# Scaling one weight on ScalarE instead of VectorE, in a kernel of five chained stages

## The chip, the cores and the metric

The kernel runs on one core of a Trainium2 chip. A core has five engines with an instruction queue each, and each of them works through its queue in order: TensorE (PE in the profile) multiplies matrices, VectorE (DVE) and ScalarE (ACT) work elementwise and also read the product banks (PSUM), GpSimd (POOL) works elementwise on the on-chip memory (SBUF) and issues gathers, and SyncE (SP) issues the other transfers (DMAs). Engines wait for one another through semaphores.

The metric is the time of one execution in microseconds (us); less is better. Before the change it is 2020.08 us, the median of three runs (2018.74 to 2021.53).

## What is computed

The reference takes `x` of shape 2 x 2048 x 512 (two sequences, 2048 tokens, 512 channels), all in float32, and adds two residual branches. Cut to what matters here:

```
y  = clip((x * style) @ weight.T * dcoef + bias)      # stage 1, modulated linear layer
hs = recurrence(rms_norm(y), 4 projections) + y       # stage 2, gated linear recurrence
up = gelu(rms_norm(hs) @ mlp_gate.T) * (rms_norm(hs) @ mlp_fc.T)   # stage 3, width 1536
x2 = x + up @ out_w.T + hs                            # stage 4, "down"
w  = softmax(aw)                                      # six weights
cat = [w0*h, w1*t, w2*m, w3*n, w4*r, w5*s]            # six branches of x2, 512 channels each
h1 = silu(cat @ int_W1 + b1)                          # stage 5, first product
q  = int8(layer_norm(h1 @ int_W2 + b2))
out = x2 + (q @ int8(rhs)) * scales
```

`h`, `t` and `s` are layer norms of `x2` with gains and offsets picked by table lookups (`h` by a gather from a table of 500 rows). `m`, `n` and `r` are `x2` plus a vector for each sequence. The six factors of the softmax are multiplied into the six 512 x 512 blocks of `int_W1` once, and not into the activations.

## The kernel before, in words

The channels lie on the 128 partitions, in chunks of 128, the tokens along the free axis. Stages 1 to 4 work on slices of 1024 tokens (four slices), stage 5 on blocks of 512 tokens (eight blocks).

**A product in seven steps.** Each large product is cut into 2 x 2 blocks and done with seven block products instead of eight (Strassen's scheme in Winograd's form). A weight tile therefore holds seven slots: four loaded quarters (0 to 3), and three sums, which `combine` (L121 to L126) makes on GpSimd in four operations. The operand's blocks `B11`, `B21`, `B12` and `B22` are likewise overwritten by sums, on VectorE, at L222. `paired_in_place` (L176) writes out the order of the steps for stages 4 and 5. A step is named here by the slot of the weights that it uses. For stage 4 the order is: step 0 with `B11` into bank pair `a`, step 1 with `B21` into `b`, step 6 with `B22` into `d`, step 4 with the old `B11` into `d`, step 5 with the new `B22`, step 2 with `B12` and step 3 with the new `B21`, these last three into `a`. Between step 6 and step 4 the program gives VectorE the sum `B22 = B22 - B11`, which overwrites what step 6 reads and which step 5 needs, and after step 4 the sum `B21 = B21 - B22`.

**Stage 4, `down(s, then)` (L899), for `s` = 0 to 3.** Its four operands `op_11`, `op_21`, `op_12` and `op_22` are large tiles (128 x 3072) that are loaded anew for each slice. Three of them lie in memory zones (A, B and C) that stage 5 takes over: zone A is `op_11`, zone B is `op_12`, zone C is `op_22`. `tap` (L920) keeps partial results: after step 6, ScalarE copies the two banks of `d` into `dk` tiles (L925), and VectorE subtracts them from the residual (L929). The argument `then` hangs other work behind single steps: the small products of the conditioning vectors, and the preparation of stage 5's weights.

**The weights of stage 5's first product.** `raw(k)` (L1209) loads a 512 x 512 block of `int_W1` whole, and `quarters(first, second)` (L1215) loads two blocks into the slots of two seven-slot tiles, with eight DMAs of 256 KB on SP (L1223). Both call `scaled(k, rhs)` (L1193), which multiplies a block by its softmax factor in four VectorE instructions of 128 x 512 (L1195). Blocks 3 and 4 are loaded raw. `quarters(2, 1)` makes the first combined weight (`w_int`, for `x2` and the time branch), to which blocks 3 and 4 are added on GpSimd (L1246). The last combined weight is `quarters(5, 0)`, called from `second_weight` (L1252), which hangs behind step 4 of the last `down` (`then[3]`: `then` counts the steps in their order from 0, and step 4 is the fourth). It takes the buffers that the raw blocks 3 and 4 leave, so its loads wait for L1246.

**What comes after.** When the last `down` no longer needs a tile, the first block of stage 5 takes its place: `load(0)` (L1356) loads the block's activations into zone A (L1358), TensorE transposes them (`tr_x`, L1383) between the last steps of `down`, ScalarE copies the transposes out (L1386), VectorE forms means and variances (L1320) and the norm (L1334). GpSimd issues four gathers from the table of 500 rows (L1363), two of them into zone B. VectorE then applies the gathered gains (L1408, L1409), and TensorE begins the first product of stage 5 (`ps_h_a`).

Instructions are queued on each engine by a scheduler in the order that it finds from the program and its priorities, except where the order is written out or `tc.issue_after(ins)` places an instruction behind another one on its own engine.

Of the kernel before, what the change touches and what calls it, by code (L numbers as in the profile page):

```python
# [11 lines left out]
AF = mybir.ActivationFunctionType  # L12
ALU = mybir.AluOpType
# [37 lines left out]
def adaln_attn_ffn(ctx: ExitStack, tc: tile.TileContext, a: dict, out: bass.AP):  # L51
    nc = tc.nc
# [11 lines left out]
    def col(name, k=0, n=1):  # L64
        at = _COL[name] + k
        return cols[:, at : at + n]
# [15 lines left out]
    wsm = const.tile([P, 6], FP, name="wsm")  # L82
# [25 lines left out]
    held = {}  # L108
# [12 lines left out]
    def combine(w):  # L121

        nc.gpsimd.tensor_add(w[:, 4], w[:, 2], w[:, 3])
        nc.gpsimd.tensor_sub(w[:, 5], w[:, 4], w[:, 0])
        nc.gpsimd.tensor_sub(w[:, 2], w[:, 0], w[:, 2])
        nc.gpsimd.tensor_sub(w[:, 6], w[:, 1], w[:, 5])  # L126

    def by_chunks(w):
        return w.rearrange("(c p) o -> p c o", p=P)
# [766 lines left out]
    def tmp(name):  # L896
        return dp.tile([P, T], FP, tag="k", name=name, bufs=8)

    def down(s, then=()):  # L899
        b, t0 = divmod(s, PER_S)  # L900
        b11, b21, b12, b22 = op
        for k, t in ((0, b11), (1, b12), (3, b22), (2, b21)):
            nc.sync.dma_start(t, pp_d[s][:, k])

        res = []
        for o in range(C):
            t = dp.tile([P, S], FP, tag="res", name=f"res_{s}_{o}", bufs=4)
            nc.sync.dma_start(t, hs_d[s][:, o, :])
            for k, half in enumerate((a_, b_)):
                x = xr[2 * (o % 2) + k]  # L910
                nc.sync.dma_start(x, by_chunks(a["xT"][b])[:, o, ts(2 * t0 + k, T)])
                nc.vector.scalar_tensor_tensor(
                    t[:, half], t[:, half], col("L0_attn_out_b", o), x, ALU.add, ALU.add
                )
            res.append(t)

        def pair(f):
            return lambda *x: [f(u, *(y[u] if y is not None else None for y in x)) for u in (0, 1)]

        def tap(n, ps, less):  # L920
            kept = []
            for u in (0, 1):
                t = tmp(f"dk{n}")
                if n == 4:
                    nc.scalar.copy(t, ps[u])  # L925
                else:
                    o, half = {1: (u, a_), 2: (u, b_), 3: (u + 2, b_)}[n]
                    if less:
                        nc.vector.tensor_sub(less[u], res[o][:, half], less[u])  # L929
                        nc.vector.tensor_add(t, ps[u], less[u])  # L930
                    else:
                        nc.vector.tensor_add(t, ps[u], res[o][:, half])
                kept.append(t)
            return kept

        def store(o, half, ps, other):
            nc.vector.tensor_add(other, ps, other)
            nc.sync.dma_start(scratch[2 * s + (half is b_)][:, o, :], other)

        return paired_in_place(  # L940
            w_dn, [b11], [b21], [b12], [b22],
            lambda n: [
                (d_ps if n == "d" else ab_ps).tile([P, T], FP, tag="s", name=f"dn_{s}_{n}{u}")
                for u in (0, 1)
            ], tap,
            pair(lambda u, ps, kept: store(u, a_, ps, kept)),
            pair(lambda u, ps, kept: store(u, b_, ps, kept)),
            pair(lambda u, ps: store(u + 2, a_, ps, res[u + 2][:, a_])),
            pair(lambda u, ps, kept: store(u + 2, b_, ps, kept)), then,
        )  # L950
# [237 lines left out]
    def block_of(k):  # L1188
        return a["int_W1"][k * D : (k + 1) * D, :].rearrange("(c p) o -> p c o", p=P)

    bias = w3.tile([P, D], FP, name="bias", bufs=1)

    def scaled(k, rhs):  # L1193
        for c in range(C):
            nc.vector.tensor_scalar(rhs(c), rhs(c), wsm[:, k : k + 1], None, ALU.mult)  # L1195

    def vectors(of):

# [10 lines left out]
    def raw(k):  # L1209
        w = w14(f"int_w1_{k}")  # L1210
        nc.sync.dma_start(w[:, 0:C], block_of(k))
        scaled(k, lambda c: w[:, c, :])
        return w

    def quarters(first, second):  # L1215


        ws = [w3.tile([P, 7, 2, 2 * P], FP, tag="w", name=f"w_int_{first}_{g}") for g in (0, 1)]
        views = []
        for at, k in enumerate((first, second)):  # L1220
            for g in (0, 1):
                for h in (0, 1):
                    nc.sync.dma_start(  # L1223
                        ws[g][:, 2 * h + at],
                        block_of(k)[:, 2 * g : 2 * g + 2, ts(h, 2 * P)],
                    )
            views.append(lambda c, at=at: ws[c // 2][:, at : at + 3 : 2, c % 2, :])
            scaled(k, views[-1])
        return ws, views[0]

    def vectors_as_operands(w):
# [5 lines left out]
    w3_4 = [raw(3), raw(4)]  # L1237
    vectors_as_operands(w3_4[0])
    w_int, of_x = quarters(2, 1)
    of_34 = [lambda c, w=w: w[:, c, :] for w in w3_4]  # L1240

# [8 lines left out]
            combine(w)  # L1250

    def second_weight():  # L1252
        ws, _ = quarters(5, 0)
        for w in ws:
            combine(w)
        w_int.extend(ws)
# [99 lines left out]
    def load(i):  # L1356
        x2T = block("x2T", i)
        nc.sync.dma_start(x2T, scratch[i])  # L1358
        return {"x2T": x2T}
# [265 lines left out]
    with tc.high_priority():  # L1625
        k = load(0)
# [64 lines left out]
    for i in range(NB):  # L1691
# [27 lines left out]
        last, k = k, nxt  # L1719
# [68 lines left out]
```

## Time and profile before

| what | us |
|---|---|
| median of three runs | 2020.08 |
| time of the profiled execution | 2021.65 |
| its span, first to last instruction | 2019.9 |
| TensorE busy in the span | 2001.7 (99%) |
| VectorE busy | 1174.8 (58%) |
| ScalarE busy | 653.4 (32%) |
| GpSimd busy | 153.8 (8%) |
| mean granted TensorE clock | 0.996 |

The profile shows one execution. "Busy" counts the time in which an engine had an instruction at work; the figures of TensorE are modelled for pipelined matmuls, and busy does not mean full speed. The granted clock is the share of full speed that TensorE was given. A row of a timeline names the start, the duration, the engine, the line, the operation, the tiles and the count; in brackets stands how long the engine had been idle before it, and what ended that. A row with a count covers several instructions. A float32 matmul of 128 x 512 shows as two records of some 0.43 us each, so that a step of `down`, twelve matmuls, is 24 records and some 10.3 us.

The stretch that the change touches is the last call of `down`, from about 1320 us to 1395 us of the span:

| engine | from 1331 us to 1352 us | from 1352 us to 1370 us |
|---|---|---|
| TensorE | steps 6 and 4 into `dn_d` | waits, then step 5 into `dn_a` |
| VectorE | scalings of the last weight, one L929 | two operand sums (L222), one L929 |
| ScalarE | two copies of `dn_d` (L925) | nothing |
| GpSimd | additions to the first weight (L1246), its `combine` | `combine` of the last weight |
| SP | loads of the last weight (L1223) | load into zone A (L1358), stores of results |

### The profile page before, as it was taken

The numbers are of one execution on the slowest core, as the hardware profiler recorded it, in microseconds if no ns is written. First come the engines' busy times: TensorE is split into PE (matmuls) and PEld (weight loads), VectorE is DVE, ScalarE is ACT, GpSimd is POOL, SyncE is SP. The second block draws the span as 40 slices with busy tenths as digits, with TensorE's granted clock in tenths as the row PEclk, the third lists the DMA queues.
The fourth block names the chain that finished last, engine by engine and source line by source line (L and its number), as shares of the span: only waits on it lengthen the run. The fifth ranks groups of instructions, "written<-read, shape, count | busy, mean of one in ns | idle before, by whom it ended". The sixth has DMA issues, their size and how long they took to land.

```text
span 2019.9 us, 16905 instructions
## 1 busy us (share of the span) xinstructions
PE 2001.7 (99%) x6292; PEld 1067.4 (53%) x6300; DVE 1174.8 (58%) x1783; ACT 653.4 (32%) x863; POOL 153.8 (8%) x127
## 2 busy tenths in 40 slices
PE   9999999999999999999999999989999999999998
PEld 5444444444444444444444444435877777777774
DVE  6667666666534224324325465466687687687675
ACT  4557777777522222222221000001302302302301
POOL 0141000000400000000010000061300000000000
PEclk9999999999999999999999999999999999999999
DMA  5661212121512112111335766533211211211110
GB/s 202 217 198 52 90 62 98 42 94 58 161 42 91 45 42 94 42 42 52 110 112 180 229 220 224 201 111 130 92 45 63 76 51 63 73 53 63 32 32 21
DMA packets 99332, 197.21 MB, mean 98 GB/s; under 512 B 21393, under 2 KB 49591, under 8 KB 95153
## 3 DMA queue, kind: packets, MB, share of 16 engines
q1 hardware_dynamic: 94584, 179.31, 26.4%
q0 software_dynamic: 4608, 16.78, 2.5%
q8 instruction: 50, 0.82, 0.2%
q14 instruction: 34, 0.27, 0.0%
q10 hardware_dynamic: 56, 0.03, 0.0%
HBM read 133.27 MB, written 58.75 MB: 95 GB/s over the span
## 4 chain that ended last, share of the span: by engine, by line
PE 95%; DVE 1%; issue 1%; POOL 1%; DMA 1%; ACT 0%; SPq 0%; POOLq 0%; ACTq 0%; DVEq 0%
PE up_a L134 16%; PE ps_h_a L134 11%; PE rec_a L134 11%; PE up_d L134 8%; PE dn_a L134 7%; PE ps_h_d L134 6%; PE rec_d L134 5%; PE ps_o L1524 5%; PE up_b L134 4%; PE dn_d L134 3%; PE ps_h_b L134 3%; PE y_a L134 3%; PE rec_b L134 3%; PE dn_b L134 2%; PE y_d L134 1%; PE ps_f L1548 1%
## 5 line engine op out<-in xcount | busy, mean ns | idle before, releaser
L134 PE MATMUL dn_a<-op,w_dn 128*128 128x512 f32 x384 | 169.7, 600 | 5.3 <-DVE op L222 5.3
L134 PE MATMUL up_a<-h,w_up 128*128 128x512 f32 x384 | 172.6, 592 | 0.0
L814 DVE SCALAR_TENSOR_TENSOR prod<-up_d,cols,k 128x512 f32<-128x512 f32 x48 | 36.0, 751 | 199.6 <-ACT k L297 199.6
L297 ACT COPY k<-up_a 128x512 f32<-128x512 f32 x144 | 84.0, 584 | 196.8 <-PE up_a L134 196.7
L794 ACT ACTIVATE gate<-gate,cols 128x512 f32<-128x512 f32 x96 | 68.8, 721 | 215.3 <-DVE gate L793 213.3
L134 PE MATMUL up_a<-h2T,w_up 128*128 128x512 f32 x288 | 129.5, 592 | 0.0
L134 PEld LDWEIGHTS dn_a<-op,w_dn 128*128 128x128 f32 x384 | 72.9, 192 | 95.8 <-issue 87.9
L134 PEld LDWEIGHTS up_a<-h,w_up 128*128 128x128 f32 x384 | 72.9, 190 | 91.9 <-issue 89.7
L134 PE MATMUL rec_a<-h,w_rec 128*128 128x512 f32 x256 | 115.1, 592 | 0.0
L134 PE MATMUL rec_a<-hT,w_rec 128*128 128x512 f32 x256 | 115.1, 592 | 0.0
L1524 PE MATMUL ps_o<-int_w,h 128*128 128x512 f32 x224 | 103.6, 605 | 0.0
L134 PEld LDWEIGHTS up_a<-h2T,w_up 128*128 128x128 f32 x288 | 54.7, 190 | 68.9 <-issue 68.9
L134 PE MATMUL up_b<-h,w_up 128*128 128x512 f32 x192 | 86.3, 592 | 0.0
L134 PE MATMUL up_d<-h,w_up 128*128 128x512 f32 x192 | 86.3, 592 | 0.0
L134 PE MATMUL dn_d<-op,w_dn 128*128 128x512 f32 x192 | 83.7, 594 | 0.0
L134 PEld LDWEIGHTS rec_a<-h,w_rec 128*128 128x128 f32 x256 | 48.6, 190 | 61.2 <-issue 61.2
L134 PEld LDWEIGHTS rec_a<-hT,w_rec 128*128 128x128 f32 x256 | 48.6, 190 | 61.2 <-issue 61.2
L297 ACT COPY k<-rec_a 128x512 f32<-128x512 f32 x96 | 55.7, 580 | 71.1 <-PE rec_a L134 69.5
L793 DVE TENSOR_TENSOR gate<-up_b,k 128x512 f32<-128x512 f32 x48 | 32.9, 690 | 72.2 <-PE up_b L134 71.2
L134 PE MATMUL up_d<-h2T,w_up 128*128 128x512 f32 x144 | 65.2, 592 | 0.0
L1524 PEld LDWEIGHTS ps_o<-int_w,h 128*128 128x128 f32 x224 | 40.2, 189 | 46.5 <-issue 46.5
L222 DVE TENSOR_TENSOR op<-op,op 128x3072 f32<-128x3072 f32 x16 | 55.8, 3486 | 12.3 <-PE dn_d L134 6.5
(403 smaller groups left out, 3444.4 us busy)
## 6 DMA issues: line engine op xcount, KB each, us to landing
pp_d<-prod SPq DMA_DIRECT2D x48, 512.0 KB
op<-pp_d SPq DMA_DIRECT2D x16, 1536.0 KB
y_d<-y SPq DMA_DIRECT2D x16, 512.0 KB
h<-y_d SPq DMA_DIRECT2D x4, 2048.0 KB
yr<-y_d SPq DMA_DIRECT2D x16, 512.0 KB
hs_d<-yr SPq DMA_DIRECT2D x16, 512.0 KB
h<-hs_d SPq DMA_DIRECT2D x4, 2048.0 KB
op<-in_xT SPq DMA_DIRECT2D x32, 256.0 KB
```

Of the source, the lines that this page charges most:

```text
L134: ins = nc.tensor.matmul(ps, ws[k // 2][:, slot, k % 2, ts(u, P)], xs[k], start=(first and k == 0), stop=(last and k == n - 1), skip_group ...
L222: nc.vector.tensor_sub(t, p, q)
L297: nc.scalar.copy(t, ps)
L793: nc.vector.tensor_add(gate[u][:, half], ps, kept)
L794: nc.scalar.activation(gate[u][:, half], gate[u][:, half], AF.Gelu, bias=col("L0_attn_mlp_gate_b", fs[u]),)
L814: nc.vector.scalar_tensor_tensor(prod[u][:, b_], ps, col("L0_attn_mlp_fc_b", fs[u]), kept, ALU.add, ALU.add)
L1524: nc.tensor.matmul(ps, h1[:, c, ts(j, P)], w2[:, c, :], start=(c == 0), stop=(c == C - 1))
L1548: nc.tensor.matmul(ps, qT[:, ts(c, P)], rq[:, c, :], start=(c == 0), stop=(c == C - 1))
```

## The change

The four instructions for each of the two blocks of the last combined weight (`quarters(5, 0)`), eight in all, are issued to ScalarE as `activation` with the function Identity and the factor as its scale, and are placed behind the copy of the second bank of `dn_d` (L925) in ScalarE's queue. `tap` records that copy in `held["dk"]`; since `tap` runs in each call of `down` and for two banks in each, what `second_weight` finds there is the last one, of `s = 3`. The other weights are scaled on VectorE as before. Both forms multiply the same values by the same factor in float32.

```diff
@@ tap, in down
                 if n == 4:
-                    nc.scalar.copy(t, ps[u])
+                    held["dk"] = nc.scalar.copy(t, ps[u])
                 else:
@@ scaled
-    def scaled(k, rhs):
+    def scaled(k, rhs, behind=None):
+
         for c in range(C):
-            nc.vector.tensor_scalar(rhs(c), rhs(c), wsm[:, k : k + 1], None, ALU.mult)
+            if behind is None:
+                nc.vector.tensor_scalar(rhs(c), rhs(c), wsm[:, k : k + 1], None, ALU.mult)
+            else:
+                with tc.issue_after(behind.ins):
+                    nc.scalar.activation(rhs(c), rhs(c), AF.Identity, scale=wsm[:, k : k + 1])
@@ quarters
-    def quarters(first, second):
+    def quarters(first, second, behind=None):
...
-            scaled(k, views[-1])
+            scaled(k, views[-1], behind)
@@ second_weight
-        ws, _ = quarters(5, 0)
+
+        ws, _ = quarters(5, 0, held["dk"])
```

In the instruction streams of the two programs, TensorE, GpSimd and SP have the same instructions in the same order. VectorE loses the eight scalings, which stood behind the copy of the bias (L1207) and around the first L929 of the last `down`, and ahead of its first operand sum there. ScalarE gains the eight, behind the two L925 copies of `s = 3` and ahead of the first copy of `tr_x` (L1386). Some waits that VectorE and GpSimd had met through the scalings are now written at later instructions: the second operand sum waits itself for the load of its tile, and the first gather names a wait for VectorE beside the one for TensorE.

## The prediction

> **What bounds the kernel now.** I read the share of busy time first, then TensorE's own waits over the whole span, then the timeline of each engine around the largest of them.
>
> ```profile
> PE 95%; DVE 1%; issue 1%; POOL 1%; DMA 1%; ACT 0%; SPq 0%; POOLq 0%; ACTq 0%; DVEq 0%
> ```
>
> The chain that ended last is TensorE for 95% of the span: only what lets TensorE wait, or lets it run slower, can move the time. TensorE's waits, longest first (total us, times, longest):
>
> ```profile
> PE dn_a L134 <- DVE op L222: 5.3, 1, 5.3
> PE ps_f L1548 <- DVE pw L1618: 3.9, 2, 3.4
> ```
>
> The largest is one wait of 5.3 us, in the last call of `down` (`s = 3`): step 5 of its product (into `dn_a`) waits for the operand sum at L222. TensorE there (start, duration, count):
>
> ```profile
> 1331.14 20.87 PE L134 MATMUL dn_d<-op,w_dn 128*128 128x512 f32 x48
> 1357.33 12.79 PE L134 MATMUL dn_a<-op,w_dn 128*128 128x512 f32 x24 [5.32 <-DVE op L222]
> 1369.95 1.04 PE L1383 MATMUL tr_x<-ident,zone_A 128*128 128x128 f32 x8
> ```
>
> The first row is steps 6 and 4, the second is step 5, which needs `op_22` minus `op_11`. VectorE in the same stretch:
>
> ```profile
> 1338.77 2.84 DVE L1195 TENSOR_SCALAR w_int<-w_int,wsm 128x512 f32<-128x512 f32 x2 [6.79 <-POOL w_int L1246]
> 1343.58 2.07 DVE L1195 TENSOR_SCALAR w_int<-w_int,wsm 128x512 f32<-128x512 f32 x2 [1.97 <-DMA w_int<-in_int_W]
> 1345.57 1.75 DVE L929 TENSOR_TENSOR dk<-res,dk 128x512 f32<-128x512 f32 x1
> 1347.24 5.70 DVE L1195 TENSOR_SCALAR w_int<-w_int,wsm 128x512 f32<-128x512 f32 x4
> 1352.86 4.41 DVE L222 TENSOR_TENSOR op<-op,op 128x3072 f32<-128x3072 f32 x1
> ```
>
> The reader is to see that the eight scalings of the last weight stand ahead of the sum in VectorE's queue. They wait for their loads, each runs beside GpSimd, and the sum is issued 11 us after its own input was free: step 6 (24 of the 48 matmuls) ends near 1331.14 + 10.50 = 1341.64. (10.50 is what this same release took one call earlier: step 6 began at 1254.92, its sum at 1265.42, and no TensorE wait followed.) The wait also cost clock, which the stage table shows (TensorE's granted clock is the third number from the end):
>
> ```profile
> 1354.00:1355.00 1.00, 0.00 (x0) 0.00 (x0) 1.00 (x1) 0.00 (x0) 1.00 (x2) 1.00 0.00 0
> 1358.00:1359.00 1.00, 1.00 (x2) 0.33 (x1) 1.00 (x2) 0.00 (x0) 1.00 (x2) 0.50 0.49 74
> 1362.00:1363.00 1.00, 1.00 (x3) 0.38 (x2) 1.00 (x1) 0.00 (x0) 1.00 (x1) 1.00 0.00 0
> ```
>
> **The change part by part.**
>
> *Removed from VectorE: eight scalings, 2.84 + 2.07 + 5.70 = 10.6 us, with their waits.* VectorE's order is then the copy of the bias (L1207, over at 1332), L929, the sum for step 5, L929, the sum for step 3. The first L929 needs ScalarE's copy of the first bank (1336.60 + 0.58 = 1337.2), so it is over by 1339. The sum starts at 1341.64 and takes 3.35 us alone (L222 at 1326.88) or 4.41 beside GpSimd: over at 1345.0 to 1346.1. TensorE can use it from 1331.14 + 20.69 = 1351.83 (48 such matmuls took 20.70 from 1143.74 to the next start). It has 5.7 us to spare, so the wait goes: 1357.33 - 1351.83 = **5.5 us**.
>
> *The clock that goes with it.* From step 5's start to the next work, 1369.95 - 1357.33 = 12.62 us passed; the 24 matmuls take 10.30 at full clock (1266.10 to 1276.40). So **2.3 us** is lost at clock 0.50. [...] The trace has the clock at half from about 1355 to 1361.8, of which TensorE worked 4.5 us, and by its matmuls lost 2.3: 7.8 in all. [...]
>
> *Added to ScalarE: eight ACTIVATEs, 128x512 each, behind the second L925 copy (over at 1341.75 + 0.58 = 1342.33).* No such instruction (SBUF to SBUF, one scale per partition) is in the trace. Nearest:
>
> ```profile
> L794 ACT ACTIVATE gate<-gate,cols 128x512 f32<-128x512 f32 x96 | 68.8, 721 | 215.3 <-DVE gate L793 213.3
> ```
>
> From SBUF, with one operand per partition: 721 ns. The squares of L396, without such an operand, took 621; L601 with two and from PSUM 777. I take 0.72, so 5.8 us (5.0 to 6.2). The loads of this weight are over by 1346 (the DMA share is 0.71 from 1345 to 1346, 0.00 after); with the last pair behind them the scaling ends near 1348. [...] By the uncontended row (0.48 us for the same scaling, L1195 at 1195 us) that is 3.8 us against 5.8, and 2 us lost if ScalarE were on the chain. But the rows of this place have 1.48 as the median of the eight, and ScalarE is idle from 1342.33 to 1371.03, when it copies `tr_x`. The eight lie wholly in that gap, at no cost; even at 1.5 us each they would end by 1355. The changed stream shows no table load among them.
>
> *GpSimd's combination of the same weight* now waits for ScalarE. Its rows:
>
> ```profile
> 1351.22 1.44 POOL L123 TENSOR_TENSOR w_int<-w_int 128x512 f32<-128x512 f32 x1
> 1354.02 4.37 POOL L125 TENSOR_TENSOR w_int<-w_int 128x512 f32<-128x512 f32 x1
> 1366.93 1.27 POOL L126 TENSOR_TENSOR w_int<-w_int 128x512 f32<-128x512 f32 x1
> 1382.46 1.30 POOL L1363 DMA_INDIRECT zone_B<-in_pw,idx_pw  x1 [14.27 <-PE dn_a L134]
> ```
>
> It first asks for the scaled values at 1351.22, or later now, for both long sums fall on GpSimd's earlier work. Beside such a sum one operation takes 4.37 us instead of 1.27. That happens twice before and twice after, so the total stays: 16 x 1.27 + 2 x 3.1 + 2 x 0.45 (beside L929) = 27.4 from 1339.9, ending near 1367 (now 1368.2). Behind it on GpSimd are the four gathers of L1363; they wait for step 2 of TensorE, which would end 7.8 earlier, at 1374.6. 7 us are spare.
>
> *What is late next.* The transposes of `tr_x`, due at 1351.83 + 10.30 = 1362.1, need the load into `zone_A` (L1358, the place of `op_11`), which SP issued at 1357.34 behind the late sum. Now step 4 frees that tile last, near 1352.1. The load's bytes were over 4.5 us after issue (DMA share 0.44 in the microsecond up to 1362, 0.00 after): 1356.6, 5 us early. SP has nothing in between, its last weight load being issued at 1342.4. The four stores of L938 and all later loads hang on VectorE's results of steps 5, 2 and 3 and move with them. The new DMA wait at the second sum is for the load of `op_21`, issued at 1308.93 and long landed.
>
> From there the chain is rigid: step 2, gather (7.4 us), VectorE's norm, two waits of 0.34 and 0.81 at `gain`, then the blocks. All of it starts from TensorE's own progress.
>
> **Sum.** 5.5 + 2.3 = 7.8 us. The profiled execution had a span of 2019.9 and a time of 2021.65: it becomes 2012.1 and 2013.9. The median of the runs shown is 2020.08, 1.6 below that execution; less 7.8 it is **2012.3 us**.
>
> **The rivals.**
>
> *The next release comes late (partial gain).* If the `zone_A` load needed 11.5 to 13.5 us instead of 4.5, or GpSimd ended at 1376 to 1378.4, 4 to 6.4 us of gain would stay: about 2015. For it: two transfers start earlier than before. Against: the 5 and 7 us to spare. 9%.
>
> *The gain is hidden (within 0.2%).* What TensorE gains up to the gathers is worth nothing unless they start earlier. If GpSimd ended at 1379 to 1386, it, not step 2, would release them: 2017 to 2024. For it: GpSimd is busy without a break from 1329.56 to 1368.2 and meets two sums of 4.4 us. Against: it idled 14.27 us before the gathers. 9%.
>
> *GpSimd becomes the bound (slower).* Place: the first gather; price: each us by which GpSimd ends after 1382.46; it decides from there, and shows as over 0.2% past 1386.5. Were all eight combinations of this weight held to 4.37 us, starting at 1353, they would end at 1388: +5.5, 2025.6. For it: I know of no row with a long run of ScalarE beside GpSimd on the same tile. Against: the copy of L925 at 1341.75 ran beside GpSimd in 0.58, its usual time, and ScalarE is done before most of these combinations. 4%.
>
> *The change doesn't do what it says:* if the scaling still stood ahead of the sum nothing would change; the changed streams have it on ScalarE behind the second L925 copy, and the other queues keep their order. Counted with the hidden gain.
>
> **How the numbers follow.** Forecast 78%, 2012.3, from 2010.5 (the runs shown spread 1.4 about their median) to 2014. The range for 8 in 10 reaches to the partial case: 2010 to 2016. Faster: 0.78 + 0.09 = 0.87; same (0.2% is 4 us, about what a measurement of this kernel can tell): 0.09; slower 0.04.
>
> **What would show it.** TensorE's wait at `dn_a` for L222 is gone, and the granted clock stays 1.00 from 1352 to 1362; the sum starts near 1341.6; eight ACTIVATEs of about 0.72 end near 1348; the first gather starts near 1374.6, still released by `dn_a`. It is wrong if `tr_x` waits for a DMA, or if the gathers start as soon as GpSimd's last combination ends.

## The result, and the profile after

| | before | after |
|---|---|---|
| median of six runs, us | 2019.41 (2016.83 to 2021.53) | 2011.33 (2009.98 to 2014.16) |
| ratio | | 0.9964, 95% interval 0.9954 to 0.9973 |
| span of the profiled execution, us | 2019.9 | 2012.4 |
| its time, us | 2021.65 | 2014.16 |

The kernel is faster by 8.1 us by the medians, by 7.5 us in the two profiled spans, and the interval of the ratio allows 5.5 to 9.3. The forecast was 7.8.

TensorE's waits in the changed kernel, the longest first (total us, times, longest):

```profile
PE ps_f L1554 <- DVE pw L1624: 3.9, 2, 3.4
PE idle L372 <- DVE ones L330: 1.0, 1, 1.0
PE ps_f L1554 <- DVE mv L1327: 1.0, 1, 1.0
```

The wait for L222, 5.3 us and first in this list before, is no longer in it. What leads now are two waits at the very end and one at the very start (L372), all of which were there before. (Behind the changed lines, line numbers are higher by 5 or 6.) TensorE's timeline around the place:

```profile
1331.58 20.87 PE L134 MATMUL dn_d<-op,w_dn 128*128 128x512 f32 x48
1352.28 10.46 PE L134 MATMUL dn_a<-op,w_dn 128*128 128x512 f32 x24
1362.58 1.04 PE L1389 MATMUL tr_x<-ident,zone_A 128*128 128x128 f32 x8
```

Steps 6 and 4, then step 5 directly behind them, in 10.3 us instead of 12.6. The start of step 6 differs by some tenths from one profiled execution to the next (1331.14 before, 1331.58 here), so I measure from there: to the first `tr_x` it was 38.81 us before (1369.95 - 1331.14), and it is 31.00 now. That is 7.81 less. The granted clock (third number from the end) stays at 1.00 where it was 0.50 before; two of the six rows that were read between 1352 and 1363 us:

```profile
1354.00:1355.00 1.00, 1.00 (x4) 0.52 (x3) 0.00 (x0) 0.00 (x0) 1.00 (x2) 1.00 0.86 311
1360.00:1361.00 1.00, 1.00 (x4) 0.51 (x3) 0.00 (x0) 0.00 (x0) 1.00 (x2) 1.00 0.65 236
```

VectorE and then ScalarE and GpSimd, from their timelines of the changed kernel:

```profile
1337.65 1.83 DVE L929 TENSOR_TENSOR dk<-res,dk 128x512 f32<-128x512 f32 x1 [5.24 <-ACT dk L925]
1342.18 4.09 DVE L222 TENSOR_TENSOR op<-op,op 128x3072 f32<-128x3072 f32 x1 [2.70 <-PE dn_d L134]
1346.20 1.76 DVE L929 TENSOR_TENSOR dk<-res,dk 128x512 f32<-128x512 f32 x1
1347.88 4.42 DVE L222 TENSOR_TENSOR op<-op,op 128x3072 f32<-128x3072 f32 x1
```

```profile
1342.67 1.34 ACT L1200 ACTIVATE w_int<-w_int,wsm 128x512 f32<-128x512 f32 x2
1344.23 3.90 ACT L1200 ACTIVATE w_int<-w_int,wsm 128x512 f32<-128x512 f32 x6 [0.23 <-DMA w_int<-in_int_W]
1363.66 1.01 ACT L1392 COPY zone_C<-tr_x 128x1024 f32<-128x1024 f32 x1 [15.53 <-PE tr_x L1389]
```

```profile
1357.05 1.26 POOL L123 TENSOR_TENSOR w_int<-w_int 128x512 f32<-128x512 f32 x1
1365.86 1.27 POOL L126 TENSOR_TENSOR w_int<-w_int 128x512 f32<-128x512 f32 x1
1375.09 1.30 POOL L1369 DMA_INDIRECT zone_B<-in_pw,idx_pw  x1 [7.96 <-PE dn_a L134]
```

The sum now waits for step 6 alone ("<-PE dn_d") and is over at 1346.3, 6 us ahead of its use. ScalarE is done with its eight at 1348.1, 9 us before GpSimd first asks for them, and then idles 15.5 us. GpSimd is done at 1367.1 and idles 8 us ahead of the gathers, which `dn_a` still releases.

### The profile page after: what moved, and what is told of

The parts are those of the page before. It is cut to its first block, busy times and chain, and to the rows that moved or that the text cites. A ratio compares the mean times of both kernels' runs of the same rounds, so it can differ in the third digit from the quotient of the medians.

```text
span 2012.4 us, 16909 instructions
## 1 busy us (share of the span) xinstructions
PE 1998.8 (99%) x6292; PEld 1066.6 (53%) x6300; DVE 1162.8 (58%) x1775; ACT 658.9 (33%) x871; POOL 152.3 (8%) x127
## 4 chain that ended last, share of the span: by engine, by line
PE 96%; POOL 1%; DVE 1%; issue 1%; DMA 0%; ACT 0%; POOLq 0%; ACTq 0%; DVEq 0%
PE up_a L134 16%; PE ps_h_a L134 11%; PE rec_a L134 11%; PE up_d L134 8%; PE dn_a L134 7%; PE ps_h_d L134 6%; PE rec_d L134 5%; PE ps_o L1530 5%; PE up_b L134 4%; PE dn_d L134 3%; PE ps_h_b L134 3%; PE y_a L134 3%; PE rec_b L134 3%; PE dn_b L134 2%; PE y_d L134 1%; PE ps_f L1554 1%
## 5 line engine op out<-in xcount | busy, mean ns | idle before, releaser
L222 DVE TENSOR_TENSOR op<-op,op 128x3072 f32<-128x3072 f32 x16 | 55.4, 3464 | 15.5 <-PE dn_d L134 9.7
```

The lines of the kernel that those rows point to most:

```text
L222: nc.vector.tensor_sub(t, p, q)
```

## The experiments

The theory: the whole gain is TensorE's wait for the sum (5.5 us) and the clock that the wait cost (2.3 us), because eight instructions stood ahead of that sum in VectorE's queue. Who executes them counts for nothing while there is cover. The ratios below are to runs of the kernel before on the same chip.

| kernel | median, us | ratio, 95% interval | step 6 to first `tr_x`, us |
|---|---|---|---|
| changed kernel | 2011.33 | 0.9964 (0.9954 to 0.9973) | 31.0 |
| `e1_order` | 2013.28 | 0.9963 (0.9949 to 0.9976) | 31.0 |
| `e2_warm` | 2016.93 | 0.9988 (0.9980 to 0.9996) | 36.7 |
| `e3_pool5` | 2012.63 | 0.9961 (0.9947 to 0.9974) | 31.0 |
| `e3_pool12` | 2020.41 | 1.0004 (0.9996 to 1.0013) | 31.0 |
| `e4_k5_act` | 2016.18 | 0.9987 (0.9978 to 0.9996) | 37.2 |
| `e4_k0_act` | 2011.55 | 0.9965 (0.9952 to 0.9979) | 31.6 |
| `e5_act16` | 2011.47 | 0.9964 (0.9950 to 0.9977) | 31.0 |

### Is it the engine or the place in the queue? (`e1_order`)

```diff
@@ sums, in paired_in_place
-                nc.vector.tensor_sub(t, p, q)
+                held["sum"] = nc.vector.tensor_sub(t, p, q)
@@ scaled, with behind
-                    nc.scalar.activation(rhs(c), rhs(c), AF.Identity, scale=wsm[:, k : k + 1])
+                    nc.vector.tensor_scalar(rhs(c), rhs(c), wsm[:, k : k + 1], None, ALU.mult)
@@ second_weight
-        ws, _ = quarters(5, 0, held["dk"])
+        ws, _ = quarters(5, 0, held["sum"])
```

> The eight scalings are back on VectorE, but queued behind the operand sum that step 5 waits for. Theory (only the place in VectorE's queue counts): the sum starts near 1342 as in the changed kernel, TensorE does not wait at dn_a, the scalings take about 1.4 us each beside GpSimd and end near 1358, GpSimd's combination ends near 1368, the first gather still waits for dn_a near 1375: 2011 to 2012 us. Rival (the gain comes from relieving VectorE and GpSimd of each other, or from ScalarE as the better engine): half the gain or less, 2015 us or more, with the first gather released by GpSimd's own combination.

Measured: 0.9963, the changed kernel's ratio. VectorE's timeline:

```profile
1342.26 3.83 DVE L222 TENSOR_TENSOR op<-op,op 128x3072 f32<-128x3072 f32 x1 [2.97 <-PE dn_d L134]
1346.01 11.33 DVE L1200 TENSOR_SCALAR w_int<-w_int,wsm 128x512 f32<-128x512 f32 x8
1357.26 4.42 DVE L222 TENSOR_TENSOR op<-op,op 128x3072 f32<-128x3072 f32 x1
```

The same eight instructions, on the old engine, at 11.33 / 8 = 1.42 us each beside GpSimd, cost next to nothing once they stand behind the sum. TensorE met one new wait of 0.3 us (for L932, which came later on VectorE). The first gather, still released by `dn_a` after 6.2 us of idle GpSimd, came 0.6 us later after step 6 than in the changed kernel, and by the end of the span 0.8 us were lost. The rival, that relief between VectorE and GpSimd or the choice of ScalarE carries the gain, falls. (The median of these five runs lies 2 us above the changed kernel's. Of that, 0.5 us is in the kernel before as well, whose median was 2019.94 beside them; the five spread over 5.2 us, so the timed runs do not tell a difference of 1 us.)

### How much of it is clock? (`e2_warm`)

```diff
     def second_weight():
+        warm = tr_A[0].tile([P, 2, D], FP, tag="tr", name="warm")
+        with tc.issue_after(held["ins"].ins):
+            for _ in range(12):
+                nc.tensor.matmul(warm[:, 0, 0:2 * P], ones, w_dn[0][:, 0, 0, :], start=True, stop=True)
         ws, _ = quarters(5, 0)
```

> The kernel before with twelve matmuls of 128x256 on constants and weights (results unused) in the gap before step 5, some 5.2 us of TensorE work. The sum stays late. Theory (wait 5.5 plus clock 2.3): step 5 starts near 1357.3 as before, runs at full clock in 10.3 instead of 12.6 us, and the kernel gains 2.3 us: 2017.1. Rival (the clock costs nothing of the end, the whole 7.8 is the late sum): no gain, 2019.4. [...]

Measured: 2016.93, ratio 0.9988, a gain of 2.4 us (0.8 to 4.0). TensorE's timeline:

```profile
1351.74 5.34 PE L1256 MATMUL warm<-w_dn,ones 128*128 128x256 f32 x24
1357.33 10.57 PE L134 MATMUL dn_a<-op,w_dn 128*128 128x512 f32 x24 [0.25 <-DVE op L222]
1367.73 1.04 PE L1387 MATMUL tr_x<-ident,zone_A 128*128 128x128 f32 x8
```

Step 5 still starts at 1357.33, for the sum is as late as ever. But it now takes 10.40 us to the first `tr_x` instead of 12.62. The granted clock is 1.00 throughout, with TensorE at work in both of these rows:

```profile
1356.00:1357.00 1.00, 1.00 (x6) 0.60 (x4) 1.00 (x1) 0.00 (x0) 1.00 (x1) 1.00 0.00 0
1360.00:1361.00 1.00, 1.00 (x4) 0.51 (x3) 1.00 (x1) 0.00 (x0) 1.00 (x2) 1.00 1.00 426
```

So of the 7.8 us, 2.2 belong to the clock and 5.6 to the wait. The timed interval, 0.8 to 4.0, is too wide to fix the size; the rows do.

### Where does GpSimd become the bound? (`e3_pool5`, `e3_pool12`)

```diff
         for w in ws:
             combine(w)
+        for _ in range(5):      # 12 in the second kernel
+            nc.gpsimd.tensor_sub(ws[1][:, 6], ws[1][:, 1], ws[1][:, 5])
```

> The changed kernel with GpSimd's last subtraction repeated five times (same values), ahead of the gathers: 5 x 1.27 = 6.4 us. Theory (7.7 us are idle there): the combination ends near 1373.5, the first gather still waits for dn_a, 2011.3 us. Rival (GpSimd is already the bound, or within a microsecond or two of it): 2013 to 2018 us.

> The same with twelve repeats, 15.2 us. Theory: GpSimd ends near 1382.4, 7.5 us after dn_a's release at 1374.9; the first gather starts there, and the end moves by 7.5: 2018.8 us. Rival (the gathers have cover behind them, something else sets the start of stage 5): less than 4 us of it shows, 2015 us or below.

Five repeats cost nothing: GpSimd idled 0.90 us before the gathers instead of 7.96, and `dn_a` still released them:

```profile
1374.83 1.12 POOL L1371 DMA_INDIRECT zone_B<-in_pw,idx_pw  x1 [0.90 <-PE dn_a L134]
```

Twelve gave the whole gain back: 2020.41, ratio 1.0004. GpSimd and TensorE of `e3_pool12`:

```profile
1366.79 16.30 POOL L1263 TENSOR_TENSOR w_int<-w_int 128x512 f32<-128x512 f32 x12
1383.25 1.09 POOL L1371 DMA_INDIRECT zone_B<-in_pw,idx_pw  x1 [0.17 <-issue]
```

```profile
1381.27 5.42 PE L134 MATMUL dn_a<-op,w_dn 128*128 128x512 f32 x12 [1.83 <-DVE dk L930]
...
1400.30 0.61 PE L1450 MATMUL gain<-zone_C,tables 30*128 30x512 bf16 x2 [4.49 <-DVE tT L1455]
1401.50 0.61 PE L1450 MATMUL gain<-zone_C,tables 30*128 30x512 bf16 x2 [0.59 <-DVE tT L1455]
1402.04 5.72 PE L134 MATMUL ps_h_a<-tT,w_int 128*128 128x256 f32 x16
```

The gathers start when GpSimd's repeats end, no longer with `dn_a`, and TensorE waits for what comes of them. The rival's mechanism is thus real; the changed kernel only stands 8 us away from it. In the profiled execution its price was more than the 7.5 us expected: the span is 8.9 us longer (2020.8 against 2012.4, from a step 6 that started 0.5 us earlier). By the two ratios it is 8.1, with some 2 us either way, which does not exclude 7.5. The repeats also held VectorE up, whose pairs of L1342 (the norm, L1340 in the changed kernel) took 2.98 us instead of 1.00, so that a step of `dn_a` waited 1.83 for L930. And during the second wait (4.49 us, from 1395.8) the granted clock fell, to 0.50 from 1399.3 to 1406.1: the matmuls of `ps_h_a` took 5.72 us instead of 3.72.

### Half of the move (`e4_k5_act`, `e4_k0_act`)

```diff
@@ quarters; first kernel, then second
-            scaled(k, views[-1], behind)
+            scaled(k, views[-1], None if at else behind)
...
+            scaled(k, views[-1], behind if at else None)
```

> Only the first block's four scalings are on ScalarE; the second block's four stay on VectorE, ahead of the sum. Theory: these four need loads that land near 1345 and take 1.4 us each, so the sum runs from about 1350.7 to 1355.1, and TensorE, due at 1352.3, waits 2.8 us. The idle time is shorter than the before kernel's 5.3 us; if the clock holds, the time is 2.8 above the changed kernel's: 2014.1 us; if it halves as before, 2016.4. Rival (any scaling ahead of the sum costs the whole 7.8): 2019 us.

> Only the second block's four scalings are on ScalarE; the first block's four stay on VectorE ahead of the sum, where they run at 1338.8 to 1345.7 as before. Theory: then L929 to 1347.4, the sum to 1351.9, TensorE due at 1352.3: no wait, or a few tenths: 2011.3 to 2011.8 us, although half of the work stays where it was. Rival (the gain is in proportion to what is moved): half of it, 2015.4 us.

The two halves are not worth the same. With the second block's four on ScalarE the ratio is 0.9965, all of the gain: the four left on VectorE fit ahead of the sum, which ends 0.3 us late:

```profile
1348.28 4.42 DVE L222 TENSOR_TENSOR op<-op,op 128x3072 f32<-128x3072 f32 x1
1352.75 10.57 PE L134 MATMUL dn_a<-op,w_dn 128*128 128x512 f32 x24 [0.34 <-DVE op L222]
```

With the first block's four on ScalarE it is 0.9987, a third of the gain. In `e4_k5_act` the whole stretch lies 3.8 us earlier in the span (step 6 at 1327.75), so its rows are read from there. VectorE and TensorE:

```profile
1342.73 5.76 DVE L1197 TENSOR_SCALAR w_int<-w_int,wsm 128x512 f32<-128x512 f32 x4 [7.23 <-DMA w_int<-in_int_W]
1348.41 4.41 DVE L222 TENSOR_TENSOR op<-op,op 128x3072 f32<-128x3072 f32 x1
```

```profile
1352.88 12.26 PE L134 MATMUL dn_a<-op,w_dn 128*128 128x512 f32 x24 [4.26 <-DVE op L222]
1364.98 1.04 PE L1389 MATMUL tr_x<-ident,zone_A 128*128 128x128 f32 x8
```

The four wait 7.23 us for their loads, and the sum waits behind them. I had the loads 1.6 us too early (the scaling began 15.0 us after the start of step 6, not 13.4), so the wait is 4.3 instead of 2.8 us. And of the two branches of the expectation, the one in which the clock halves came true: 1364.98 - 1352.88 = 12.10 us, 1.8 more than at full speed. That the median came to 2016.18, beside the 2016.4 expected for this branch, is in part luck: the wait was 1.5 us longer and the loss of clock 0.5 us smaller than in that sum. The stage table of this kernel (TensorE's granted clock is the third number from the end):

```profile
1352.00:1353.00 1.00, 0.12 (x1) 0.12 (x2) 1.00 (x2) 0.00 (x0) 1.00 (x1) 1.00 0.00 0
1354.00:1355.00 1.00, 1.00 (x3) 0.37 (x2) 1.00 (x2) 0.00 (x0) 1.00 (x1) 0.50 0.69 172
1356.00:1357.00 1.00, 1.00 (x2) 0.34 (x1) 1.00 (x1) 0.00 (x0) 1.00 (x1) 0.50 0.97 410
1358.00:1359.00 1.00, 1.00 (x4) 0.41 (x3) 0.83 (x1) 0.00 (x0) 1.00 (x1) 1.00 0.00 0
```

Here the clock was 1.00 while TensorE waited (until 1352.88), and 0.50 only from 1354.0 on, when it was back at work. By the rows this half-move costs 37.2 - 31.0 = 6.2 us against the changed kernel. The two ratios put it at 4.6, each with some 2 us either way: they agree, but don't fix the size. The thirteen runs of this kernel spread over 9.8 us (2011.77 to 2021.55), more than those of any other here; why is not shown.

### What does ScalarE's price matter? (`e5_act16`)

```diff
                     nc.scalar.activation(rhs(c), rhs(c), AF.Identity, scale=wsm[:, k : k + 1])
+                    nc.scalar.activation(rhs(c), rhs(c), AF.Identity, scale=ones[:, 0:1])
```

> The changed kernel with each of ScalarE's eight scalings followed by one more of the same shape with the factor 1 (same values): ScalarE's work for this weight doubles, by 8 x 0.65 = 5.2 us, ending near 1353.4. Theory (GpSimd first asks for it at 1357): no change, 2011.3 us. [...]

Measured: 0.9964, no difference. ScalarE's sixteen ended at 1352.05, and GpSimd asked for them at 1356.4:

```profile
1350.72 1.33 ACT L1201 ACTIVATE w_int<-w_int,ones 128x512 f32<-128x512 f32 x2
1356.40 1.26 POOL L123 TENSOR_TENSOR w_int<-w_int 128x512 f32<-128x512 f32 x1
```

## Why the prediction was right, point by point

- **The wait, 5.5 us.** Gone. Step 5 starts 20.70 us after step 6 instead of 26.19: 5.5. `e1_order` shows that the place in VectorE's queue is the cause, and `e4_k0_act` that it is the finish of the sum before TensorE is due, and not the amount of work moved.
- **The clock, 2.3 us.** `e2_warm` measured 2.2 with the wait still in place. The sum with the loss read from the row, 7.8, fits the 7.81 measured in the rows: the clock was at 0.50 for 6.8 us, 4.5 us of which TensorE worked (last section). The 2.3 is what one profiled execution lost; what other executions of the kernel before lose is not shown.
- **ScalarE, 0.72 us each, ending near 1348, hidden.** The eight took 0.71 each (0.70 to 0.72), overlapped a little, and ended at 1348.1. Doubling them cost nothing. Neither engine's price was on the path, only what stood behind it.
- **GpSimd's total unchanged, ending near 1367, gathers still released by `dn_a` near 1374.6.** It ended at 1367.1, and the gathers began at 1375.1, 0.44 of which is the later start of step 6. That there were 7 us to spare is shown by the runs with repeats, of which 5 fitted and 12 did not.
- **The load into `zone_A` is 5 us early.** SP issued it at 1352.48, expected near 1352.1, and `tr_x` did not wait.
- **The rigid chain behind it.** Counted from step 6, the 7.81 us at `tr_x` were 8.25 at the second half of the first `ps_h_a`: VectorE waited 6.97 instead of 7.43 us for the gathered rows (neither is the whole time of a gather, which the forecast took the 7.4 for: from the first issue to VectorE's start it was 9.10 before and 8.63 after), and with that the wait of 0.34 at `gain` went. They stayed 8.25 to 8.26 up to the seventh block of stage 5, where TensorE met a wait that the kernel before does not have, and were 7.95 from there to the end. Less the 0.44 by which step 6 started later, that is the 7.5 of the spans.

```profile
1830.80 1.09 PE L1349 MATMUL tr_h<-ident,pw 128*128 128x128 f32 x8 [0.26 <-ACT lnT L1352]
```


The rivals: the late `zone_A` load and the hidden gain did not come about. GpSimd as the bound did not either, but can be made to, at the place predicted, and costs somewhat more by the rows than predicted since VectorE and the clock pay too. What the forecast left out are the two small terms of the last point, +0.44 and -0.30 us.

No version here beats the changed kernel: in this stretch TensorE has no wait left but 0.8 us at `gain`, and the longest ones now lie in the last 20 us of the kernel.

## What to carry to other kernels

When TensorE waits for one instruction of another engine, look at what stands ahead of that instruction in its engine's queue, and at when its own inputs were ready: here the sum's were ready 11 us before it ran. Work that is needed late can be put behind it on the same engine or moved to an idle one, and both gave the same here to within 1 us; all that mattered was that the late sum ended before TensorE was due and that the moved work ended before its own reader asked. Price a wait of TensorE with the clock lost beside it (here 2.3 us with a wait of 5.3, 1.8 with one of 4.3), and measure the slack of each engine behind the moved work: a queue with 8 us of cover took 6.7 us more at no cost, and gave the whole gain back at 16.

## What the runs showed of the hardware that was not expected

In three stretches the granted clock was at half for 6.8, 3.4 and 6.8 us, and fell 3.0, 5.4 and 3.5 us after the start of TensorE's wait. With stage tables cut at 0.2 us, it was 0.50 from 1355.0 to 1361.8 before (6.8 us; the wait began at 1352.0), from 1354.0 to 1357.4 in `e4_k5_act` (3.4 us, beginning 1.1 us after TensorE had resumed; the wait began at 1348.6), and from 1399.3 to 1406.1 in `e3_pool12` (6.8 us; the wait began at 1395.8). The rows at the edges, a pair for each:

```profile
1355.00:1355.20 0.20, 0.00 (x0) 0.00 (x0) 0.20 (x1) 0.00 (x0) 0.20 (x1) 0.53 0.00 0
1361.80:1362.00 0.20, 0.20 (x2) 0.19 (x1) 0.20 (x1) 0.00 (x0) 0.20 (x1) 0.91 0.00 0
```

```profile
1353.80:1354.00 0.20, 0.20 (x2) 0.16 (x1) 0.20 (x1) 0.00 (x0) 0.20 (x2) 0.99 1.80 246
1357.40:1357.60 0.20, 0.20 (x1) 0.03 (x1) 0.20 (x1) 0.00 (x0) 0.20 (x1) 0.98 0.01 0
```

```profile
1399.20:1399.40 0.20, 0.00 (x0) 0.00 (x0) 0.20 (x1) 0.00 (x0) 0.00 (x0) 0.76 0.99 184
1406.00:1406.20 0.20, 0.20 (x2) 0.16 (x1) 0.20 (x1) 0.00 (x0) 0.00 (x0) 0.68 0.95 399
```

In the first two, what was lost was about half of the part in which TensorE worked: 4.5 us of the 6.8 before (2.3 lost), all of the 3.4 in `e4_k5_act` (1.8 lost). So a wait of 5.3 us went with 6.8 us of half clock, and one of 4.3 with 3.4.

One VectorE multiplication of 128x512 took 0.48 us with GpSimd idle (the kernel before, from 1195 us) and 1.42 to 1.48 between GpSimd's operations (`e1_order` and the kernel before), while each of GpSimd's grew only from 1.27 to 1.45. Against the long sum it was the other way round: the sum grew from 3.35 to 4.42, and the GpSimd operation caught by it from 1.27 to 4.38 (the changed kernel).

The first 14 us of the program differ between the profiled executions, though nothing was changed there: the first matmuls of `y_a` start at 12.91 us in the kernel before, 13.17 in the changed kernel, 13.41 in `e1_order` and 12.92 in `e3_pool12`, and at 9.60 in `e4_k5_act`. Most of the difference is TensorE's own pace: the 20 small matmuls just ahead (`idle`, L372) took 4.61 us in the changed kernel and 2.48 in `e4_k5_act`, with the granted clock read as 1.00 in both. The cause is open. That alone is 3.6 us, nearly half of this change's effect, which is why the rows were measured from the start of step 6. Whether it is also what spreads the timed runs of one kernel (2016.58 to 2021.95 for the kernel before) is not shown.
